# The product of two weight matrices of a one-head attention layer, as seven products of half-size blocks

## The chip, the cores and the metric

The kernel runs on one core of a Trainium2 chip. The metric is device microseconds of one execution. A core has a matrix engine (TensorE, PE in the profile; its weight loads are listed as PEld), VectorE (DVE), ScalarE (ACT), GpSimd (POOL), and SyncE (SP), which here only issues transfers (DMA). Each engine takes its own instructions in order and waits on semaphores for the others. Before the change the kernel took 2408.46 us, the median of 3 runs (2408.44 to 2410.81).

## The reference

Four layers act on x (4 images, 512 channels, 32 x 32 positions, so 1024 tokens each), all in float32:

- layer 0: attention with 8 heads of 64, an output projection, and x added;
- layer 1: linear attention (softplus of queries and keys), a gate from the maximum and the mean of x, and x added;
- layer 2: layer norm over channels, attention with one head of 512, an output projection, and x added;
- layer 3: group norm, attention with 4 heads of 128, an output projection, and x added.

The change is in layer 2, whose core is

```
xn = (xf - mu) * rsqrt(var + EPS) * norm_w
q, k, v = split(xn @ w_qkv.T + b_qkv)
out = softmax(q @ k.T * scale) @ v
out = out @ w_proj.T + b_proj
return x + out
```

With one head, the value and the output weights can be multiplied once, ahead of all tokens: out = softmax(..) @ (xn @ W) with the 512 x 512 matrix W = (w_proj @ w_v).T. Query and key weights can be put together in the same way. Both are done in the kernel.

## The kernel before, in words

plain_path computes everything for one image after another, layer by layer; 512 x 512 matrices are kept as 4 chunks of 128 partitions. PE's order of work is written out by hand (manual_schedule, line 1754): the order of the program text is PE's order. The other engines' order comes from a scheduler that places each instruction by priority and by when its inputs are expected, with two means to steer it: soon() (line 679) raises the priority of what it encloses, and issue_after(i) lets instructions follow instruction i.

**Seven products.** Large matrix products are made from seven half-size block products instead of eight, with sums before and after. seven_products (line 728) holds the scheme. The sums of one operand, the "weights", are made by block_sums or sum_weights (lines 718 and 708), four tensor operations on POOL (lines 711, 712, 714, 715). The sums of the other operand, the "inputs", are made by sum_inputs (line 698), four operations on DVE: L701 the first sum, L702 the second, which needs the first, L703 the third, and L704 the fourth. sum_inputs also records its last instruction in summed[0]. The products are p1 to p7. p1 and p2 need no sums; ACT copies their results out (L763, L768, or L770 with a bias). p6 needs the second sum of both operands, p7 the third, p5 the first, p4 the fourth; the results of p3 to p7 are joined on DVE: L791 (p6), L797 (p7) and L754 or L756 (p5, p4 and p3). The order is p1 and p2 of the output blocks, then for each pair of blocks p6, p7, p6, p5, p4, p7, p3, p5, p4, p3. A matmul with float32 operands shows as two PE instructions in the trace.

**Slots.** Other work is threaded between products: pieces is a list of small functions, and each call of slot() runs the next one; idle is a function that does nothing and takes a slot. later is a list of work with a countdown in ticks; tick() counts it down. layer_norm (line 1578) and linear_attention (line 1389) return such lists of pieces.

**Around the change** (lines 1804 to 1858). Layer 0 of the last image has just ended; the last image's layer 1 and the first image's layer norm are still to be done, and they are interleaved with two products of weights:

1. gq, the product of the query and key weights: four times fold (line 1804: four matmuls 128 x 128 x 512 that add up in one PSUM bank; PE line L654), then a copy by ACT (L1846). Three of the folds come early, the fourth here. After the third and the fourth copy there is a slot.
2. hv, the product of the value weights (the last third of w2) and the output weights wo2: four folds (L654, "acc<-wo,w" in the trace), each with a copy by ACT (L1853) and a slot.
3. two weighted biases, uq and bo2 (weighted_bias, line 550; DVE line L559), which issue_after(summed[0]) puts after the last instruction of the sums made last.
4. the first image's layer 2: the query product with gq (seven_products with two slots, "acc<-ln,gq" and "acc<-w,ws" on PE line L724), then the product of the tokens with hv (project_v), then the attention (one_head).

The pieces in the slots are: the rest of the layer norm of the first image (the reciprocal L1614 and the scaling L1619 of its first half; centering L1597, squares on ACT L1602, their sum L1606, and the matmul that adds over channels L1611 of its second half), the gate of the last image (gates: on DVE a maximum over all tokens, L1418, on ACT four sums, L1421), its features (two matmul groups, L654 "feat<-x,block" and L1404), the transposes of its tokens (L1437 on DVE, then transfers to squares and from there to l, L1445 and L1451 on SP), and so on. L1103 is the end of layer 0 of the last image on DVE. Line 1830 loads a copy of half an image for the second image's layer norm.

Buffers: PSUM has four one-bank tiles (acc) and two two-bank tiles (sc). The POOL sums of seven_products lie in the two buffers of tag "sum". The tag "os" has one buffer; it holds sums of layer 0's output weights until layer 0 is over, and later sums of layer 2's queries.

Of the kernel before, what the change touches and what calls it, by code (L numbers as in the profile page):

```python
# [13 lines left out]
F32 = mybir.dt.float32  # L14
# [4 lines left out]
P = 128  # L19
B = 4  # L20
C = 512
S = 1024
NC = C // P
# [452 lines left out]
def plain_path(ctx: ExitStack, tc: tile.TileContext, d: dict, out: bass.AP, count):  # L476
# [11 lines left out]
    nc = tc.nc  # L488
# [4 lines left out]
    work = ctx.enter_context(tc.tile_pool(name="work", bufs=1))  # L493
# [6 lines left out]
    def acc_tile():  # L500
        return ps_acc.tile([P, TB], F32, tag="acc", name="acc")
# [24 lines left out]
    def chunks_tile(tag, name, bufs=1):  # L526
        return work.tile([P, NC, TB], F32, tag=tag, bufs=bufs, name=name)
# [7 lines left out]
    def load_wo(src):  # L535
        t = wpool.tile([P, NC, C], F32, tag="wo", name="wo")
        nc.sync.dma_start(t, src.rearrange("(c p) o -> p c o", p=P))
        return t
# [112 lines left out]
    def product(ps, lhs, rhs):  # L651

        for c in range(NC):
            nc.tensor.matmul(ps, lhsT=lhs(c), rhs=rhs(c), start=(c == 0), stop=(c == NC - 1))  # L654
# [3 lines left out]
    later, pieces = [], []  # L658
# [7 lines left out]
    def tick():  # L666
        for item in later:
            item[0] -= 1
        while later and later[0][0] <= 0:
            later.pop(0)[1]()  # L670

    def slot():
        tick()
        if pieces:
            pieces.pop(0)()

    idle = lambda: None
# [20 lines left out]
    def sum_inputs(tiles, inputs):  # L698

        t = tiles  # L700
        nc.vector.tensor_tensor(t[0], inputs(0, 1), inputs(0, 0), ALU.subtract)  # L701
        nc.vector.tensor_tensor(t[1], inputs(1, 1), t[0], ALU.subtract)  # L702
        nc.vector.tensor_tensor(t[2], inputs(1, 1), inputs(0, 1), ALU.subtract)  # L703
        last = nc.vector.tensor_tensor(t[3], inputs(1, 0), t[1], ALU.subtract)  # L704
        summed[:] = [last.ins]
        return t
# [16 lines left out]
    def tokens_moving(ps, w, x, m, o, start, stop):  # L723
        nc.tensor.matmul(  # L724
            ps, lhsT=w[:, m, :], rhs=x[:, m, :], start=start, stop=stop, skip_group_check=True
        )
# [152 lines left out]
    def project_qkv(wqkv, bias, src, vt, room, first=False, between=lambda: None):  # L879

        q = q_tiles()
        k = work.tile([P, NC, S], F32, tag="k", name="k")
        inputs = lambda j, tb: src(tb)[:, 2 * j : 2 * j + 2, :]
        made = []

        def sums():
            with tc.issue_after(closing.pop()) if closing else nullcontext():
                made.extend(sum_inputs([pt_tile("t") for _ in range(4)], inputs))
            return made


        seven_products(
            NC,
            lambda i, j, o: wqkv[:, 2 * j : 2 * j + 2, i * C + o * P : i * C + (o + 1) * P],
            inputs,
            lambda i, o: col(bias, i * NC + o),
            lambda i, tb, o: k[:, o, bass.ts(tb, TB)] if i else q[tb][:, o, :],
            sums,
            slots=1,
            first=first,  # L900
        )

        assert len(pieces) <= 7
        wv = wqkv[:, :, 2 * C :]
        between()
        project_v(vt, wv, inputs, made, room())
        return q, k

    def output_sums(wo):

        t = work.tile([P, 4, NC // 2, C // 2], F32, tag="os", bufs=1, name="os")
        return sum_weights(
            [t[:, i] for i in range(4)],
            lambda i, j: wo[:, 2 * j : 2 * j + 2, i * C // 2 : (i + 1) * C // 2],
        )
# [838 lines left out]
    with tc.manual_schedule(engines={mybir.EngineType.PE}):  # L1754


        ps = acc_tile()
# [11 lines left out]
        for b in range(B):  # L1769
            vt = v_tiles()  # L1770
            if b > 0:
                pieces.extend(linear_attention(b - 1, lambda i: vt[i]))
            q, k = project_qkv(
                wqkv0, "bqkv0", lambda tb: xs[b][:, :, bass.ts(tb, TB)], vt,
                lambda: chunks_tile("ot", "ws"), first=(b == 0),
                between=outputs_bias,
            )
# [7 lines left out]
            if b == 0:  # L1785
                os = output_sums(wo0)
            if b == B - 1:
                w2 = wpool.tile([P, 3 * NC, C], F32, tag="wqkv", name="w2")
# [15 lines left out]
        def fold(ps, left, right, o):  # L1804
            product(ps, lambda c: w2[:, left + c, bass.ts(o, P)], lambda c: right[:, c, :])
# [19 lines left out]
        wo2 = load_wo(d["wo2"])  # L1825
# [15 lines left out]
        for o in range(NC):  # L1841
            ps = gps.get(o)
            if ps is None:
                ps = acc_tile()
# [2 lines left out]
            if o >= NC // 2:  # L1847
                slot()
        hv = w2[:, :NC, :]
        for o in range(NC):  # L1850
            ps = acc_tile()
            fold(ps, 2 * NC, wo2, o)
            nc.scalar.copy(hv[:, o, :], ps)  # L1853
            slot()

        with tc.issue_after(summed[0]):
            uq = weighted_bias("uq", loadedq)
# [5 lines left out]
        for b in range(B):  # L1863
# [18 lines left out]
            def sums():  # L1882
# [12 lines left out]
                slots=2,  # L1895
            )

            pair = lambda t, i: t[:, 2 * i : 2 * i + 2, :]
# [42 lines left out]
        for b in range(B):  # L1941
            vt = v_tiles()

            q, k = project_qkv(
                wqkv3, "bqkv3", lambda tb: ready[tb], vt,
                lambda: wpool.tile([P, NC, C], F32, tag="wo", name="ws") if b == 0
                else chunks_tile("ot", "ws"),
            )
            if b == 0:
                wo3 = load_wo(d["wo3"])  # L1950
                os = output_sums(wo3)
# [17 lines left out]
@with_exitstack  # L1969
def conv_seq(ctx: ExitStack, tc: tile.TileContext, d: dict, out: bass.AP):  # L1970
    nc = tc.nc
    flag = ctx.enter_context(tc.tile_pool(name="flag", bufs=1))
    count = flag.tile([1, 1], mybir.dt.int32, name="count")
    plain_path(tc, d, out, count)
    good = nc.values_load(count, min_val=0, max_val=P)  # L1975
    with tc.If(good < P):
        general_path(tc, d, out)
# [56 lines left out]
```

## Time and profile before

| | us |
|---|---|
| median of 3 runs | 2408.46 (2408.44 to 2410.81) |
| the profiled execution, time | 2407.96 |
| its span in the profile | 2406.2 |
| PE busy | 2396.1 |
| DVE busy | 1505.6 |
| ACT busy | 702.1 |
| POOL busy | 245.9 |
| first instruction of hv's product (L654, acc<-wo,w) | 935.02 |
| first instruction of the query's product after it (L724) | 953.42 |

Times are microseconds from the start of the span unless marked ns. A row of the timeline gives start, length, engine, source line, operation, what is written and read, the shape, the number of instructions merged, and in square brackets idle time before it with what ended it. A row of the waits gives who waited for whom, the total, the number of times and the longest. A window's row gives its length, then for each engine the busy time and the number of instructions, then the granted PE clock (1.00 is full), the share of DMA time and GB/s. Matmul ends are modelled: rows of matmuls that follow each other overlap by about 0.17 us in this list, so the pace is read from start to start. Each fence in the text is one view of the profile.

### The profile page before, as it was taken

To read this page: it belongs to the slowest core of one execution; us is meant where nothing else is said; L and a number is where in the kernel's file an instruction comes from. 1 tells how busy PE (TensorE), PEld (TensorE's weight loads), DVE (VectorE), ACT (ScalarE), POOL (GpSimd) and SP (SyncE) were. 2 spreads that over 40 slices of the span, in tenths; PEclk is the share of its full clock that TensorE was granted. 3 is DMA by queue.
4 is the path that set the end of the run, shared out by engine and by line. 5 is a ranking of instruction groups with operands and counts; after the bars stand their busy time and mean duration, and the time that the engine had idled before them with its cause. 6 is when DMAs were issued, how large, how long until landed. Compare 5 with 4: busy or idle time off the path is not lost. (4 is left out here: it accounts for less than half of the span.)

```text
span 2406.2 us, 24706 instructions
## 1 busy us (share of the span) xinstructions
PE 2396.1 (100%) x10014; PEld 1197.0 (50%) x10014; DVE 1505.6 (63%) x1834; ACT 702.1 (29%) x866; POOL 245.9 (10%) x240
## 2 busy tenths in 40 slices
PE   9999999999999999999999999999999999999999
PEld 5444544453445344544646445455556446455653
DVE  3678577757875789685585865654563554445344
ACT  1454154315531653230302202013321330331132
POOL 4001100110020001102102021011020001002000
PEclk9999999999999999999999999999999999999999
DMA  6001220212021213111002020110010001000001
GB/s 188 10 10 36 57 80 10 62 31 80 19 62 63 100 37 95 64 66 79 18 9 79 22 87 0 62 70 18 36 70 1 22 31 53 0 35 36 0 25 43
DMA packets 45895, 112.28 MB, mean 47 GB/s; under 512 B 3807, under 2 KB 21215, under 8 KB 42830
## 3 DMA queue, kind: packets, MB, share of 16 engines
q1 hardware_dynamic: 45774, 110.64, 13.7%
q8 instruction: 80, 1.31, 0.2%
q14 instruction: 41, 0.34, 0.0%
HBM read 75.79 MB, written 33.78 MB: 46 GB/s over the span
## 5 line engine op out<-in xcount | busy, mean ns | idle before, releaser
L958 ACT ACTIVATE pt<-sc 128x1024 f32<-128x1024 f32 x384 | 379.6, 1022 | 531.4 <-PE sc L953 303.9
L967 DVE TENSOR_TENSOR sum<-sum,pt 128x1024 f32<-128x1024 f32 x256 | 314.5, 1229 | 160.8 <-ACT pt L958 147.5
L984 PE MATMUL acc<-pt,v 64*64 64x512 f32 x2048 | 245.7, 591 | 0.0
L948 PE MATMUL sc<-q,k 64*64 64x512 f32 x2048 | 243.8, 591 | 1.1 <-ACT pt L958 1.1
L999 PE MATMUL acc<-pt,v 128*128 128x512 f32 x512 | 240.8, 594 | 0.0
L953 PE MATMUL sc<-q,k 128*128 128x512 f32 x512 | 239.8, 593 | 0.0
L724 PE MATMUL acc<-t,ws 128*128 128x512 f32 x384 | 173.9, 593 | 0.0
L711 POOL TENSOR_TENSOR ws<-wqkv 128x256 f32<-128x256 f32 (+1 forms) x40 | 39.2, 981 | 1289.9 <-PE acc L1035 513.3
L964 DVE TENSOR_TENSOR sum<-pt 128x1024 f32<-128x1024 f32 x64 | 78.0, 1219 | 137.0 <-ACT pt L958 137.0
L999 PEld LDWEIGHTS acc<-pt,v 128*128 128x128 f32 x512 | 96.6, 190 | 125.3 <-issue 121.6
L953 PEld LDWEIGHTS sc<-q,k 128*128 128x128 f32 x512 | 96.8, 190 | 116.2 <-issue 92.9
L984 PEld LDWEIGHTS acc<-pt,v 64*64 64x64 f32 x2048 | 76.8, 133 | 143.9 <-issue 141.5
L948 PEld LDWEIGHTS sc<-q,k 64*64 64x64 f32 x2048 | 76.4, 133 | 141.8 <-issue 132.9
L724 PEld LDWEIGHTS acc<-t,ws 128*128 128x128 f32 x384 | 72.7, 190 | 88.1 <-issue 86.3
L763 ACT COPY v<-acc 128x512 f32<-128x512 f32 x24 | 14.1, 586 | 305.1 <-PE acc L849 305.1
L693 DVE RECIPROCAL rd<-acc 128x512 f32<-128x512 f32 (+1 forms) x25 | 83.8, 3353 | 29.1 <-PE acc L1035 29.1
L763 ACT COPY q<-acc 128x512 f32<-128x512 f32 x40 | 23.4, 586 | 221.1 <-PE acc L724 221.1
L849 PE MATMUL acc<-ws,t 128*128 128x256 f32 x384 | 87.1, 380 | 0.0
L1095 PE MATMUL acc<-ot,wo 128*128 128x256 f32 x360 | 85.4, 382 | 1.7 <-DVE ot L1068 1.7
L856 PE MATMUL acc<-q,ln 128*128 128x512 f32 x192 | 86.6, 594 | 0.0
L856 PE MATMUL acc<-qs,w 128*128 128x512 f32 x192 | 86.5, 592 | 0.0
L754 DVE TENSOR_TENSOR v<-acc,v 128x512 f32<-128x512 f32 x72 | 49.7, 690 | 53.1 <-PE acc L849 53.0
(321 smaller groups left out, 3392.6 us busy)
## 6 DMA issues: line engine op xcount, KB each, us to landing
home<-x SPq DMA_DIRECT2D x8, 2048.0 KB
x<-home SPq DMA_DIRECT2D x8, 2048.0 KB
rds<-quotients SPq DMA_DIRECT2D x32, 256.0 KB
squares<-squares SPq DMA_DIRECT2D x32, 256.0 KB
out<-x SPq DMA_DIRECT2D x31, 256.0 KB
rds<-quotients SPq DMA_DIRECT2D x7, 1024.0 KB
x<-in_x SPq DMA_DIRECT2D x3, 2048.0 KB
v<-squares SPq DMA_DIRECT2D x12, 512.0 KB
```

Of the source, the lines that this page charges most:

```text
L693: nc.vector.reciprocal(rd, ps)
L724: nc.tensor.matmul(ps, lhsT=w[:, m, :], rhs=x[:, m, :], start=start, stop=stop, skip_group_check=True)
L849: nc.tensor.matmul(ps[:, bass.ts(r, C // 2)], lhsT=x[:, m, bass.ts(2 * o + r, P)], rhs=w[:, m, :], start=(start and r == 0), stop=stop, sk ...
L856: nc.tensor.matmul(ps, lhsT=x[:, m, bass.ts(o, P)], rhs=w[:, m, :], start=start, stop=stop, skip_group_check=True,)
L948: nc.tensor.matmul(ps[half(h), s, :], lhsT=key(g, i)[half(s), half(h)], rhs=q[qb][half(s), g, :], start=True, stop=True,)
L953: nc.tensor.matmul(ps[:, s, :], lhsT=key(g, 2 * i + s), rhs=q[qb][:, g, :], start=True, stop=True)
L958: exps.append(nc.scalar.activation(pt, ps, AF.Exp, scale=scale).ins)
L964: adds.append(nc.vector.tensor_tensor(acc, pts[n - 1], pt, ALU.add).ins)
L967: adds.append(nc.vector.tensor_tensor(acc, acc, pt, ALU.add).ins)
L984: nc.tensor.matmul(outs[qb, g][r][half(s), :], lhsT=v[i // 2][half(r), i % 2, g * P + s * hd : g * P + (s + 1) * hd], rhs=pt[half(r), s, : ...
L999: nc.tensor.matmul(outs[qb, g][0], lhsT=v[j // 2][:, j % 2, bass.ts(g, P)], rhs=pt[:, s, :], start=(j == 0), stop=(j == NT - 1),)
L1095: nc.tensor.matmul(ps[i][:, bass.ts(o, n)], lhsT=w[:, m, bass.ts(o, P)], rhs=t[:, m, :], start=(start and m + o == 0), stop=(stop and m == ...
```

## The change

The four folds of hv are replaced by a call of seven_products. The weights operand is the value part of w2, in 128 x 128 blocks (sums on POOL, 128 x 256 elements for each of two output blocks); the inputs operand is wo2, split in halves by rows and by columns, so that the moving side of a matmul has 256 columns. The four sums of wo2 go to a new tile fsums in the buffer of tag "os" (L701 to L704 on DVE, 128 x 512 elements each). There is no bias, so p1 and p2 are copied by ACT (L763, L768) and the rest are joined by DVE with 128 x 256 elements each (two L791, two L797, six L754). PE does 28 matmuls of 256 columns instead of 16 of 512.

The slots are one in the first part and five in the second, six where there were four; two idle pieces are put into the list, so the other pieces up to there are the same. Since sum_inputs sets summed[0], the weighted biases uq and bo2 now follow the sums of wo2; before, summed[0] was an instruction of layer 0.

In the order of instructions the first transpose (L1437) of the second pair now stands on DVE ahead of the maximum L1418, the sums of wo2 stand between the additions of the squares (L1606), and the bias rows L559 stand after the sums. On PE the feature matmuls (L654, "feat<-x,block") stand after p1, p2 and the first p6, p7, p6, p5; before, they stood after the second fold. On SP the load of line 1830 stands ahead of the four loads L1451; before, it stood after them. On POOL the eight sums of the value weights stand ahead of the sums of gq.

```diff
         hv = w2[:, :NC, :]
-        for o in range(NC):
-            ps = acc_tile()
-            fold(ps, 2 * NC, wo2, o)
-            nc.scalar.copy(hv[:, o, :], ps)
-            slot()
+
+        pieces[1:1] = [idle]
+        pieces[3:3] = [idle]
+        n, pair = C // 2, NC // 2
+        fsums = work.tile([P, 4, pair, n], F32, tag="os", bufs=1, name="fs")
+        columns = lambda tb: slice(tb * n, (tb + 1) * n)
+        inputs = lambda j, tb: wo2[:, pair * j : pair * (j + 1), columns(tb)]
+        seven_products(
+            pair,
+            lambda i, j, o: w2[
+                :, 2 * NC + pair * j : 2 * NC + pair * (j + 1), bass.ts(i * pair + o, P)
+            ],
+            inputs,
+            None,
+            lambda i, tb, o: hv[:, i * pair + o, columns(tb)],
+            lambda: sum_inputs([fsums[:, k] for k in range(4)], inputs),
+            None,
+            lambda ps, *args: tokens_moving(ps[:, :n], *args),
+            lambda ps: ps[:, :n],
+            slots=1,
+        )
 
         with tc.issue_after(summed[0]):
             uq = weighted_bias("uq", loadedq)
             bo2 = weighted_bias("bo2", loadedv)
```

## The prediction

> **What bounds the kernel now.** I read the engine totals first, then the waits of the matrix engine (PE), then the busy time of each engine stage by stage around the edited lines, then the timelines of PE and of VectorE (DVE) there. The totals, and the only row of PE's waits between 926 and 1000 us:
>
> ```profile
> PE 2396.1 (100%) x10014; PEld 1197.0 (50%) x10014; DVE 1505.6 (63%) x1834; ACT 702.1 (29%) x866; POOL 245.9 (10%) x240
> ```
> ```profile
> PE acc L724 <- DVE w L702: 0.4, 1, 0.4
> ```
>
> PE is busy for the whole span, and its waits in the whole program are five rows that add up to 4.5 us. So a delay of PE anywhere is handed on to the end: hardly any idle time later can take it up. DVE's average of 63% hides the stage that is edited. Two windows (length, then busy time of PE, weight load, DVE, ACT, POOL, then clock, DMA share, GB/s):
>
> ```profile
> 934.00:954.00 20.00, 19.89 (x47) 8.61 (x46) 20.00 (x25) 9.46 (x18) 5.13 (x8) 1.00 0.00 0
> 954.00:965.00 11.00, 10.57 (x33) 3.79 (x32) 11.00 (x11) 4.62 (x7) 5.09 (x4) 1.00 0.57 142
> ```
>
> From 934 to 965 us DVE is busy for 31.0 of 31 us, and PE too, but for the 0.4 us that it waits for DVE at the end. The timelines there (start, length, engine, line), first PE's, then DVE's:
>
> ```profile
> 935.02 7.03 PE L654 MATMUL acc<-wo,w 128*128 128x512 f32 x16
> 941.89 3.60 PE L654 MATMUL feat<-x,block 128*128 128x512 f32 x8
> 945.32 3.60 PE L654 MATMUL acc<-wo,w 128*128 128x512 f32 x8
> 949.03 1.12 PE L1611 MATMUL lnsums<-sq,ones 128*128 128x512 f32 x2
> 949.99 3.60 PE L654 MATMUL acc<-wo,w 128*128 128x512 f32 x8
> 953.42 3.60 PE L724 MATMUL acc<-ln,gq 128*128 128x512 f32 x8
> 956.95 3.65 PE L1404 MATMUL feat<-x,block 128*64 128x512 f32 x16
> 960.53 3.70 PE L724 MATMUL acc<-ln,gq 128*128 128x512 f32 x8
> 964.67 1.53 PE L724 MATMUL acc<-w,ws 128*128 128x512 f32 x3 [0.43 <-DVE w L702]
> ```
> ```profile
> 933.64 4.41 DVE L1418 TENSOR_REDUCE gate<-x 128x4 f32<-128x4096 f32 x1
> 937.97 3.33 DVE L1614 RECIPROCAL rstd<-rstd 128x512 f32<-128x512 f32 x1
> 941.23 0.62 DVE L1597 SCALAR_TENSOR_TENSOR ln<-lnsums,x 128x512 f32<-128x512 f32 x1
> 941.78 2.72 DVE L1619 SCALAR_TENSOR_TENSOR ln<-ln,cols,rstd 128x512 f32<-128x512 f32 x4
> 944.42 1.87 DVE L1597 SCALAR_TENSOR_TENSOR ln<-lnsums,x 128x512 f32<-128x512 f32 x3
> 946.22 0.68 DVE L1606 TENSOR_TENSOR sq<-sq 128x512 f32<-128x512 f32 x1
> ```
>
> The reader is to see that the product of the value and output weights (32 instructions acc<-wo,w; each matmul in the source is two) needs nothing that DVE makes here, so PE works through it while DVE does its reduction, reciprocal and layer norm. It is what PE does while DVE is behind.
>
> **The change part by part.** The sum is made against the profiled execution: 2407.96 us, of it 2406.2 us span; it stands 0.5 us under the median of the runs, 2408.46.
>
> *PE's own work.* Removed: 32 instructions of 512 columns; 16 run from 935.02 to 941.89, 0.43 us each: 13.7 us. Added: 7 products x 2 output blocks x 2 matmuls x 2 = 56 instructions of 256 columns. Rows of that form (L849) give 0.226 us each (16 from 984.57 to 988.22, 16 from 994.97 to 998.53): 12.7 us. Gain: 1.1 us.
>
> *DVE's added work.* Four sums of wo2 (L701 to L704, 128x512) at a pitch of 0.60 us, as rows of that shape start at 928.87, 929.47, 930.08: 2.4 us. Ten joins of 128x256 from PSUM, which the trace does not have: 128x256 rows in SBUF last 0.42 us (L1308), 0.34 of pitch if they overlap as the others do; 128x512 joins last 0.69 at 0.60 of pitch. Between 3.4 and 6.0 us for ten; I take 3.5, as the work goes by elements. Together 5.9 us, on an engine without a free microsecond. At most 1.6 comes back: L563 (four numbers) lasts 1.11 us and one L559 row 1.21 instead of 0.68, both beside POOL's work, which moves.
>
> *What is queued ahead of the sums.* This decides. In the changed kernel's instruction order the first sum (L701) stands on DVE behind the last L1103, one stream transpose (moved up), the reduction, the reciprocal, one L1597, four L1619, three L1597 and one L1606; the third product, p6, needs the second sum (L702). The four L559 that ran between 928.26 and 933.64 now stand behind the sums, because issue_after(summed[0]) now names the last sum of wo2. So the last two L1103 follow the PE product that ends at 930.03, and are through at 931.3 rather than 933.03. Then the transpose, 1.16 (950.73 to 951.89 before): 932.45. Reduction 4.33: 936.8. Reciprocal 3.26: 940.05. L1597, L1619, L1597 as in the rows above, 0.55 + 2.64 + 1.80: 945.05. L1606, L701, L1606, L702 at 0.60: 947.45. p6 can start at about 947.55.
>
> *When PE gets there.* p1 and p2 begin at 935.02, as the old product did: 16 instructions, 3.6 us. p2 waits for ACT's copy of p1, which stands behind two L1421 rows that end at 937.1: 0.8 us. PE is through at 939.4 and stands still until 947.55: **8.15 us**. The feat product (3.4 us) can't fill this, since PE takes its products in order and feat comes after four of the DVE-fed ones.
>
> *From there on.* p6 0.9; p7 waits 0.25 for the third sum, 948.7; p7, p6, p5 2.7: 951.4. feat 3.44: 954.9. Four products 3.6: 958.5. L1611 0.9 and two products 1.8: 961.15. There the query's product starts, 953.42 before. It takes 10.8 us to its own p6: 971.95. DVE's second reciprocal waits for L1611 and runs from 960.3 to 963.55; two joins 0.7, four L1619 2.6 to 3.8 (the latter beside POOL's work), L701, L703, L702 3.4: 970.3 to 971.5. DVE is just in time, so the 0.43 us go: 971.95 against 964.67, **+7.3 us**.
>
> *The clock.* PE's last work ends at 2400.8. What the granted clock (last column but two) does then, and the kernel's first matmul, in the form of grouped instructions (busy, mean ns):
>
> ```profile
> 2403.00:2404.00 1.00, 0.00 (x0) 0.00 (x0) 0.00 (x0) 0.00 (x0) 0.00 (x0) 1.00 0.12 35
> 2404.00:2405.00 1.00, 0.00 (x0) 0.00 (x0) 0.00 (x0) 0.00 (x0) 0.00 (x0) 0.84 0.00 0
> 2405.00:2406.00 1.00, 0.00 (x0) 0.00 (x0) 0.00 (x0) 0.00 (x0) 0.00 (x0) 0.50 0.05 16
> ```
> ```profile
> L724 PE MATMUL acc<-x,wqkv 128*128 128x512 f32 x1 | 1.2, 1191 | 0.0
> ```
>
> After 3.9 us without work the clock is half. The first matmul lasts 1191 ns, later ones 592, and they do so from about 5 us, 3.9 us after PE's first work at 1.12. So the wait should halve the clock, and 3.9 us of work at half speed lose 1.95 us, less 0.25 for p7's wait, which they cover: **+1.7 us**. Bounds: nothing if the clock stays, 3.4 if the slow stretch is twice as long.
>
> [...]
>
> *What costs nothing.* POOL's eight added sums (128x256, 0.72 us each, 5.8 in all) need only w2 and buffers that L1035 has left by 904; POOL has been idle for 206 us there; without that cover they would follow gq's first copy at 931 and end at 937, still before 947. gq's own sums move behind the last products (961) and are through by about 965, needed from 971.95; without that slack they would cost their 2.9 us. SP: L1830 (1 MB of x) moves ahead of the four L1451 loads; all wait for the squares after the second transpose, which ends at 957.05 (957.39 before), while PE is 7 us later; uncovered, the 1 MB would take some 4 us. ACT has four 128x256 copies for four 128x512.
>
> Sum: waits 8.15 + 0.8 + 0.25, less 1.1 of work, less the 0.43 and 0.36 that PE waits in this stretch now: 7.3. With the clock **+9.0 us**: 2417.0 for a profiled execution, 2417.4 against the median.
>
> **The rivals.**
> 1. *The clock stays, or its loss is hidden*: the waits alone, +7.3, 2415.8. For it: the clock falls only 3.9 us into the gap. Against: it would be half when work comes back.
> 2. *DVE is late a second time.* With the slow clock, L1611 and with it the second reciprocal come 1.7 us later, and DVE has the query's sum at 972.0 to 973.2, PE wants it at 973.65. Joins at 0.60 (+2.5) put DVE last, and more where POOL's sums run beside it: 2 to 3.5 us more, about 2420.
> 3. *Not slower.* DVE gets to the sums early. wo2 has landed by 934; if L701 and L702 ran ahead of the reduction, p6 would not wait, PE would keep 1.1 - 0.8 us, and what is left is DVE's 5.9 - 1.6 = 4.3 us ahead of the query's sum, or nothing if the bias rows go behind it: 2408.2 to 2412.7. It decides from an L702 that ends by 943.3, a gap too short for the clock and +3.0 in all. Against it: the order puts L701 behind the reduction and the reciprocal, 7.6 us, and the rows above show DVE taking them without a gap.
>
> **How the numbers follow.** Forecast 0.55, rival 1 0.20, rival 2 0.17, rival 3 0.08. A measurement can't tell less than 0.2% (4.8 us, up to 2413.3) from no change. Rival 3 gives 0.06 of same and 0.02 of faster; all else is slower, 0.92. The range reaches from 2414.2 (+5.7: rival 1, if DVE also gets its 1.6 us back ahead of the sums) to 2420.8 (rival 2, and the clock's upper bound, +12.4): it leaves out rival 3 and the tail of rival 2.
>
> **What the changed profile would show.** A wait of about 8 us of PE L724 for DVE fs L702 near 947; DVE's L701 on fs at about 945.6, behind the reduction; a granted clock under 1 around 944 to 951 and the first 256-column instructions near 0.43 us apart; the query's product at about 963; all later stages as long as before. I would be wrong with no such wait (rival 3), with a wait at a clock of 1.00 (rival 1), or with a second wait of L724 for w (rival 2).

## The result, and the profile after

The changed kernel takes 2422.73 us, the median of 6 runs (2420.23 to 2423.25), against 2408.53 us for the kernel before (6 runs, 2408.28 to 2410.81): a ratio of 1.0056, 95% interval 1.0046 to 1.0067. That is 14.2 us slower. The forecast was 9.0 us slower, 2417.4, with a range of 2414.2 to 2420.8: the direction was right, the size outside the range. The profiled execution took 2422.85 us, its span 2420.7 us.

The rows of PE's waits for the edited stretch. There was one of 0.4 before; now there are three.

```profile
PE acc L724 <- DVE fs L702: 8.2, 1, 8.2
PE acc L724 <- DVE w L702: 2.9, 1, 2.9
PE acc L724 <- ACT w L763: 0.6, 1, 0.6
```

The timeline of PE after the change, p6 to p5 of the new product, the query's first products, and the query's p6 to p5:

```profile
948.17 6.35 PE L724 MATMUL acc<-fs,ws 128*128 128x256 f32 x16 [8.20 <-DVE fs L702]
954.36 3.60 PE L654 MATMUL feat<-x,block 128*128 128x512 f32 x8
...
963.84 3.60 PE L724 MATMUL acc<-ln,gq 128*128 128x512 f32 x8
...
977.57 8.74 PE L724 MATMUL acc<-w,ws 128*128 128x512 f32 x16 [2.92 <-DVE w L702]
```

This execution is 0.44 us later than the one before when the stretch begins (first L1595 at 934.60 against 934.16). The query's product then starts at 963.84, where it started at 953.42: 10.0 us later, net of the 0.44. Its own p6 waits once more, for 2.92 us, and its 16 instructions take 8.58 us to the next row (986.15) instead of 6.94. Windows of 1 us show why both groups of 16 are long (clock in the last column but two):

```profile
943.00:944.00 1.00, 0.00 (x0) 0.00 (x0) 1.00 (x3) 0.00 (x0) 0.00 (x0) 0.66 0.00 0
...
953.00:954.00 1.00, 1.00 (x5) 0.86 (x4) 0.48 (x3) 0.00 (x0) 0.00 (x0) 0.72 0.00 0
...
977.00:978.00 1.00, 0.43 (x1) 0.46 (x2) 1.00 (x2) 0.00 (x0) 0.00 (x0) 0.73 0.00 0
...
980.00:981.00 1.00, 1.00 (x3) 0.34 (x1) 0.00 (x0) 0.98 (x2) 0.00 (x0) 0.56 0.00 0
```

All windows between the first and the second, and between the third and the fourth, have 0.50. A window of mean 0.66 at levels of 1 and 0.5 means that the clock fell 0.32 us into it. So it fell at 943.32, 3.35 us after PE's last work (939.97), and came back at 953.56, 5.4 us after work resumed. It fell a second time at 977.46, after 2.8 us without work, and came back at 980.88, 3.3 us after work resumed. The last section shows what these moments have in common.

The timeline of DVE after the change, at its two late arrivals:

```profile
946.13 0.69 DVE L701 TENSOR_TENSOR fs<-wo 128x512 f32<-128x512 f32 x1
...
947.34 0.69 DVE L702 TENSOR_TENSOR fs<-wo,fs 128x512 f32<-128x512 f32 x1
...
963.03 3.35 DVE L1614 RECIPROCAL rstd<-rstd 128x512 f32<-128x512 f32 x1 [1.15 <-ACT rstd L1613]
...
967.78 4.09 DVE L1619 SCALAR_TENSOR_TENSOR ln<-ln,cols,rstd 128x512 f32<-128x512 f32 x3
971.79 2.29 DVE L701 TENSOR_TENSOR w<-ln 128x1024 f32<-128x1024 f32 x1
974.01 2.28 DVE L703 TENSOR_TENSOR w<-ln 128x1024 f32<-128x1024 f32 x1
976.21 1.21 DVE L702 TENSOR_TENSOR w<-ln,w 128x1024 f32<-128x1024 f32 x1
```

The first arrival is as worked out: net of the 0.44, L701 starts at 945.69 and L702 at 946.90, for 945.65 and 946.85 in the forecast. At the second, the four L1619 take 4.9 us from start to start, and L701 and L703 2.2 each. In the kernel before the same rows were

```profile
957.32 3.80 DVE L1619 SCALAR_TENSOR_TENSOR ln<-ln,cols,rstd 128x512 f32<-128x512 f32 x4
961.04 1.21 DVE L701 TENSOR_TENSOR w<-ln 128x1024 f32<-128x1024 f32 x1
962.18 1.21 DVE L703 TENSOR_TENSOR w<-ln 128x1024 f32<-128x1024 f32 x1
```

POOL's timeline beside them after the change, the first and the third of four sums of the tokens' product (project_v), and then the first and the last of the same four before it:

```profile
967.94 1.71 POOL L711 TENSOR_TENSOR ws<-w 128x512 f32<-128x512 f32 x1 [0.96 <-DVE w L754]
...
971.28 1.72 POOL L712 TENSOR_TENSOR ws<-ws,w 128x512 f32<-128x512 f32 x1
```
```profile
953.73 1.27 POOL L714 TENSOR_TENSOR ws<-w 128x512 f32<-128x512 f32 x1 [13.64 <-issue]
...
957.65 1.60 POOL L715 TENSOR_TENSOR ws<-w,ws 128x512 f32<-128x512 f32 x1
```

These sums read hv, and the code puts them into the buffer of wo2. Before, they began when PE had read wo2 for the last time (its last fold ends at 953.6), ACT's last copy of hv was done by 954.21, and they ran from 953.73 to 959.25: beside the end of the reciprocal, L563, a transpose and the first of the four L1619, at 1.26 to 1.28 us each for the first three. Now hv is whole only with the last join L754 (967.45 to 967.86), and that join stands on DVE behind the second reciprocal. So they begin 14 us later, beside the rows that the query waits for.

The account up to the first matmul of L1314, in the attention that follows, at 1085.02 after and 1070.58 before: 14.4, less the 0.44, is 14.0. Waits 8.20 + 0.64 + (2.92 - 0.43); the first group of 16 took 6.19 to the next row for 3.62 at the forecast's pace, 2.57 (the slow clock and p7's wait); the second 8.58 instead of 6.94, 1.64; less 1.08 of work at the same pace, and less the 0.36 by which PE's rows from 935.02 to 953.42 before stand further apart than their work (18.40 for 18.04). Sum: 14.1.

### The profile page after: what moved, and what is told of

The parts are those of the page before. It is cut to its first block, busy times and chain, and to the rows that moved or that the text cites. A ratio compares the mean times of both kernels' runs of the same rounds, so it can differ in the third digit from the quotient of the medians.

```text
span 2420.7 us, 24782 instructions
## 1 busy us (share of the span) xinstructions
PE 2399.1 (99%) x10038; PEld 1203.8 (50%) x10038; DVE 1513.5 (63%) x1848; ACT 701.1 (29%) x866; POOL 253.9 (10%) x248
## 3 DMA queue, kind: packets, MB, share of 16 engines
q8 instruction: 81, 1.33, 0.2%
## 5 line engine op out<-in xcount | busy, mean ns | idle before, releaser
L763 ACT COPY v<-acc 128x512 f32<-128x512 f32 x24 | 14.1, 586 | 305.6 <-PE acc L849 305.6
L763 ACT COPY q<-acc 128x512 f32<-128x512 f32 x40 | 23.4, 586 | 222.7 <-PE acc L724 222.7
L849 PE MATMUL acc<-ws,t 128*128 128x256 f32 x384 | 87.1, 380 | 0.0
L754 DVE TENSOR_TENSOR v<-acc,v 128x512 f32<-128x512 f32 x72 | 49.8, 691 | 53.1 <-PE acc L849 53.0
```

The lines of the kernel that those rows point to most:

```text
L849: nc.tensor.matmul(ps[:, bass.ts(r, C // 2)], lhsT=x[:, m, bass.ts(2 * o + r, P)], rhs=w[:, m, :], start=(start and r == 0), stop=stop, sk ...
```

## The experiments

Each run is compared with runs of the kernel before on the same chip. Medians of before: 2408.79 us for the first four experiments, 2408.40 for the next four, 2408.24 for the last two. Single runs of one kernel spread by up to 3.3 us (experiment 1), so differences of a microsecond or two between medians are read together with the traces.

**1. The clock kept up.** Between p2 and p6, PE does nine products of 512 columns whose result nobody reads.

```diff
+        def busy():
+            ps = two_tile("busy")[:, 0, :]
+            for _ in range(9):
+                nc.tensor.matmul(ps, lhsT=ones, rhs=wo2[:, 0, :], start=True, stop=True)
+        pieces[0:1] = [both(pieces[0], busy)]
```

> The changed kernel with nine matmuls of 512 columns more (18 PE instructions, 7.7 us at full clock) between p2 and p6 of the weight product. They read wo2 and a matrix of ones, write a PSUM tile that nobody reads, and so fill the 8.2 us in which PE waits for the sums of wo2 without making anything later. Theory (the idle halves PE's clock, and the slow stretch after it costs 2.6 us of its own): the granted clock stays 1.00 from 940 to 956, the first sixteen 256-column instructions after the wait take 3.6 us instead of 6.2, L1611 comes 2.6 us earlier, and DVE's and POOL's chains behind it with it, so the second wait stays near 2.9 us: 2420.1 us. Rival (DVE alone sets the time through this stretch, the slow clock lies beside its bias rows and joins): what PE gains is added to the second wait, which grows to about 5.5 us, and the time stays at 2422.7 us.

Measured: 2420.24 us (2418.51 to 2421.76), ratio 1.0046 (1.0029 to 1.0063). PE's timeline in this run:

```profile
948.15 3.97 PE L724 MATMUL acc<-fs,ws 128*128 128x256 f32 x16 [0.47 <-DVE fs L702]
951.95 3.60 PE L654 MATMUL feat<-x,block 128*128 128x512 f32 x8
...
975.16 10.11 PE L724 MATMUL acc<-w,ws 128*128 128x512 f32 x16 [2.92 <-DVE w L702]
```

p6 starts at 948.15 as in the changed kernel, and feat follows 3.80 us later instead of 6.19: the slow clock of the first gap costs 2.4 us there, and 2.5 by the medians. The wait for the query's sum stays at 2.92: that wait does not come from the slow clock of the first gap, as PE and DVE move together. The slow clock behind the second gap cost this execution 3.1 us (10.11 against 7.03 at full clock), more than the 1.6 of the changed kernel, so its own time, 2421.76, is the highest of the four.

**2. POOL held back.** A one-column POOL operation reads the query's fourth sum (L704), and the four sums for project_v follow it.

```diff
...
+            if b == 0:
+                probe = small.tile([P, 1], F32, tag="probe", bufs=1, name="probe")
+                last = made[3][:, 0, :1]
+                held = tc.issue_after(nc.gpsimd.tensor_tensor(probe, last, last, ALU.add).ins)
+            with held:
+                project_v(
...
```

> The changed kernel with POOL's four sums of hv for the first image's value product (128x512, L711 to L715) held back until DVE has made the fourth sum of the query's inputs (L704): a one-column POOL operation reads that sum, and the four are queued behind it. Theory (the second wait comes from POOL and DVE working side by side: L1619, L701 and L703 take about twice their usual time there): L1619 at 0.66 to 0.7 us each, L701 and L703 at 1.2 us instead of 2.3, the sum L702 about 4 us earlier, before PE wants it, so the second wait (2.9 us) and the slow clock after it (1.6 us) both go: 2418.2 us. Rival (those DVE rows are slow for another reason, or DVE is late by its order alone): the rows keep their lengths, a second wait of 2 to 3 us stays, 2422.7 us, or more by what the later POOL sums cost the value product.

Measured: 2418.31 us (2417.86 to 2418.46), ratio 1.0040 (1.0026 to 1.0054). DVE's timeline in this run, the rows that answer to those at 967.78 and 971.79:

```profile
967.38 2.06 DVE L1619 SCALAR_TENSOR_TENSOR ln<-ln,cols,rstd 128x512 f32<-128x512 f32 x3
969.37 1.21 DVE L701 TENSOR_TENSOR w<-ln 128x1024 f32<-128x1024 f32 x1
```

The rows are half as long, the query's p6 starts at 974.09 without a wait and at full clock, and 4.4 us are gone. So the second wait, and the second fall of the clock with it, come from POOL's sums beside DVE. (A wait of 0.24 for the keys is new; experiment 7 says where it comes from.)

**3. The features' product between p2 and p6**, so that PE has work in the first gap.

```diff
-        pieces[1:1] = [idle]
-        pieces[3:3] = [idle]
+        pieces[0:2] = [both(*pieces[0:2]), idle, idle, idle]
```

> The changed kernel with the first feature matmuls (8 instructions, 3.4 us) put into the slot after p2, ahead of p6, so that real work fills part of the first wait. Theory: the first wait shrinks from 8.2 to 4.8 us; the clock still falls, 3.8 us after the last feature instruction, so the slow stretch stays; L1611 comes 3.4 us earlier, but DVE then still has its bias rows and joins to do and gains only some 2 us, and the second wait grows to between 3 and 4.5 us: 2419.3 to 2421 us. Rival (the first wait alone is the loss): all 3.4 us come back, 2419.3 us, and with a clock that stays up 2416.7 us.

Measured: 2419.14 us (2418.88 to 2419.40), ratio 1.0043 (1.0027 to 1.0060). The first wait is 4.77 instead of 8.20, as feat's 3.4 us now lie in it; the group of 16 takes 5.21 to the next row, 1.4 more than the 3.80 of experiment 1. The query's p6 starts at 973.10, 4.5 us earlier than in the changed kernel, but there the wait is 3.25, and its group takes 9.91 instead of 8.74. So 3.6 us are gone, and the loss at the query's sums is not among them. The time is the rival's, 2419.3, and just under the range of the theory; the second wait grew as the theory had it, but only by 0.33, and the first group lost 1.0 less than in the changed kernel (5.21 to the next row instead of 6.19).

**4. The sums of wo2 ahead of the reciprocal.** This is what rival 3 rests on.

```diff
+        def sums_early():
+            with tc.high_priority(offset=2000):
+                t = sum_inputs([fsums[:, k] for k in range(4)], inputs)
+            return t
...
-            lambda: sum_inputs([fsums[:, k] for k in range(4)], inputs),
+            sums_early,
```

> The changed kernel with the four sums of wo2 given a high priority, so that DVE has L701, L703 and L702 ahead of the reciprocal, directly behind the maximum L1418, and the joins come earlier too. Theory (the place of the sums in DVE's queue makes the first wait): L702 ends at about 939.5, p6 starts with a wait under 1 us, no slow clock; then the squares' sum L1606 and with it L1611 is late on DVE instead, a wait of about 2 us, and the second reciprocal follows the bias rows, so that the query's product waits 1 to 4 us for L702 beside POOL: 2411 to 2416 us. Rival (DVE's 5.9 us of added work is the loss, wherever it stands): the first wait moves whole into later waits, 2420 us or more.

Measured: 2420.26 us (2419.35 to 2421.52), ratio 1.0049 (1.0033 to 1.0066). p6 no longer waits. PE's waits in this run:

```profile
PE acc L724 <- DVE w L702: 4.7, 1, 4.7
PE lnsums L1611 <- DVE sq L1606: 4.6, 1, 4.6
```

What DVE does early, it does not do for the squares and for the query: two other waits of PE take the place of the first, and the time is less by only 2.5 us. The theory had 2411 to 2416; the rival, 2420 or more, is what came.

**5. Both: sums early, POOL held back** (the diffs of 4 and 2 together).

> The changed kernel with both moves at once: the four sums of wo2 ahead of the reciprocal on DVE, and POOL's four 128x512 sums held until DVE is through with the query's fourth sum (L704). Theory (what is lost is DVE's added work, and POOL running beside DVE lengthens it): no wait of L724 for fs; the wait of L1611 for sq stays at about 4.6 us, as it is DVE's own work ahead of it; L1619 and L701 go back to about 0.66 and 1.2 us each, so the wait of 4.7 for w falls under 1.5 us and its slow clock stretch goes: 2414 to 2416.5. Rival (POOL is incidental, the query's sums are late because DVE has had more to do): the wait for w keeps 3 us or more, 2418.5 to 2420.3.

Measured: 2415.14 us (2414.34 to 2417.47), ratio 1.0029 (1.0018 to 1.0041). The wait of L1611 is 4.59 still, and its two instructions take 2.08 instead of 1.02, so PE is slow after it; the wait for the query's sum is 0.61. So even with the order of rival 3 and without POOL beside the query's sums the kernel stays 6.7 us slower. Not all of that is DVE's added work: PE also waits 1.12 us for the keys (L1462), which comes from holding POOL back (experiments 7 and 10), and 1.5 us are slow clock behind the 4.59.

**6. The kernel before with DVE's added work alone.** PE's product stays the old one; on DVE the four sums of wo2 and ten additions of 128x256 are done, and nobody reads them.

```diff
...
             nc.scalar.copy(hv[:, o, :], ps)
+            if o == 0:
+                keep = summed[0]
+                sum_inputs([fsums[:, k] for k in range(4)], inputs)
+                summed[0] = keep
+            for k in range((2, 2, 3, 3)[o]):
+                half = hv[:, o, (k % 2) * n : (k % 2 + 1) * n]
+                nc.vector.tensor_tensor(junk, half, half, ALU.add)
             slot()
```

> The kernel before with DVE's added work alone: the four sums of wo2 are made and ten additions of 128x256 on hv that nobody reads are done on DVE between the folds; PE's instructions are those of before, and nothing waits for the added work. Theory (5.9 us on a DVE that had no free microsecond, with a rise beside POOL): L1611 late by 1 to 2.4 us and the query's second sum late by 3 to 6 us in all: 2412 to 2416. Rival (the loss is made by the product's dependence on the sums and by its form on PE, while DVE can take the work in the time that the bias rows and small rows give back): 2408 to 2410.

Measured: 2415.49 us (2414.94 to 2417.30), ratio 1.0028 (1.0017 to 1.0039), 7.1 us slower than before. PE's timeline and then DVE's, in this run:

```profile
972.71 9.20 PE L724 MATMUL acc<-w,ws 128*128 128x512 f32 x16 [5.62 <-DVE w L702]
```
```profile
958.04 1.31 DVE L1865 TENSOR_TENSOR junk<-w 128x256 f32<-128x256 f32 x1
959.28 1.75 DVE L1619 SCALAR_TENSOR_TENSOR ln<-ln,cols,rstd 128x512 f32<-128x512 f32 x1
960.96 1.49 DVE L1865 TENSOR_TENSOR junk<-w 128x256 f32<-128x256 f32 x1
```

This execution reaches the stretch 2.5 us late (first L1595 at 936.69), so its starts can't be set directly against those of before. 5.9 us of work on the full DVE come back as 5.2 us more of wait for the query's sum and 0.4 at L1611; the gap then costs 2.2 us of slow clock (9.20 against 7.03). Two of the additions, 0.41 each elsewhere, take 1.31 and 1.49 beside POOL's sums (956.58 to 962.2), so about 2 us of this belong to POOL. These additions read SBUF alone, while the joins have one input in PSUM. The scheduler's order changed too: L1381 and three of the bias rows now stand ahead of the query's L702, both transposes L1437 behind it. No product in seven blocks is needed for a loss of this size: the load on DVE, in the order that the scheduler gives it, is enough.

**7. The sums of wo2 on POOL, and POOL's later sums held back.** POOL has nothing to do from 907.6 on; its first sum of wo2 starts at 934.45, when wo2 has arrived. The diff of 2 is in this kernel too.

```diff
-            lambda: sum_inputs([fsums[:, k] for k in range(4)], inputs),
+            fsums_on_pool,
...
+        def fsums_on_pool():
+            t = [fsums[:, k] for k in range(4)]
+            tt = nc.gpsimd.tensor_tensor
+            tt(t[0], inputs(0, 1), inputs(0, 0), ALU.subtract)
...
+            return t
```

> The changed kernel with the four sums of wo2 on POOL, which is idle there, in place of DVE, and POOL's sums for the tokens' product held until L704. DVE then has only ten joins more than before, 3.5 us. Theory: p6 does not wait (POOL has the second sum by about 939), the clock stays, DVE's joins show as a wait of 1 to 2 us at L1611 or of 1 to 2 us for w, against 1.1 us less work on PE: 2407.5 to 2411. Rival (even ten joins on the full DVE cost more than they take, or POOL's sums slow DVE's maximum and reciprocal): 2413 or more.

Measured: 2411.14 us (2410.46 to 2412.89), ratio 1.0011 (1.0002 to 1.0021). PE's waits:

```profile
PE keys L1462 <- DVE block L1387: 1.8, 1, 1.8
...
PE acc L724 <- DVE w L702: 1.4, 1, 1.4
PE lnsums L1611 <- DVE sq L1606: 1.3, 1, 1.3
```

p6 doesn't wait, its group takes 3.45 to the next row (939.93 to 943.38), and 11.5 of the 14.2 us are gone. Ten joins still cost two waits of 1.3 and 1.4. The 1.8 for the keys is new, since POOL's sums now stand beside L1383 to L1386 (1.51, 1.80 and 1.69 us, and 0.67, 1.20 and 1.21 in experiment 10), steps of the softplus on DVE that the keys' transpose (L1462) waits for; with it the time lies just above the 2407.5 to 2411 of the theory.

**8. The kernel before with POOL's sums held back** (the diff of 2 alone).

> The kernel before with POOL's four 128x512 sums held until DVE is through with L704. Theory: the four L1619 take 2.7 us instead of 3.8 and the four-number L563 about 0.1 instead of 1.11, DVE is 2 us earlier at the query's second sum, and the only wait there, 0.43 us, goes: 2407.9 to 2408.6. Rival: POOL's later sums delay the tokens' product or slow the joins of the query: 2409.5 or more.

Measured: 2407.76 us (2407.33 to 2408.43), ratio 0.9997 (0.9987 to 1.0006): no difference that can be told. The rows of L1619 are shorter there too (2.70 instead of 3.80 for four) and the 0.43 us wait is gone, with 0.28 at the keys in its place. Before the change the neighbourhood of POOL and DVE cost next to nothing.

**9. Clock kept up and POOL held back** (1 and 2 together): what is left should be the forecast's sum without its clock term.

> The changed kernel with both things that the forecast missed or mis-sized taken out together: nine dummy products of 512 columns between p2 and p6 that keep the clock up, and POOL's four 128x512 sums held until L704. The dummy products lie in the wait for the sums, so the output is the same. Theory (what is left is the forecast's sum without its clock term, +7.3 us, and the two loss terms add): no slow clock in 934 to 980, no wait for w, 2415.0 to 2416.5. Rival (the two terms overlap, or a third loss lies under them): 2417.3 or more, with another wait of PE in the stretch.

Measured: 2415.82 us (2415.24 to 2417.51), ratio 1.0032 (1.0020 to 1.0044). PE's timeline:

```profile
961.13 3.60 PE L724 MATMUL acc<-ln,gq 128*128 128x512 f32 x8
...
971.78 7.03 PE L724 MATMUL acc<-w,ws 128*128 128x512 f32 x16
```

The forecast had 961.15 and 971.95 for these two rows, and DVE's L702 at 970.3 to 971.5; it ends at 970.54. The two losses add: 2.5 and 4.4 apart, 6.9 together.

**10. As 7, with POOL's sums held until the features are done**: the probe reads what L1387 writes.

```diff
...
-                last = made[3][:, 0, :1]
+                last = soft[0][:, :1]
...
```

> The changed kernel with the sums of wo2 on POOL, and POOL's four 128x512 sums held until the last instruction of the features (L1387) in place of L704. Theory (POOL beside L1383 to L1387 is what makes the keys' wait of 1.8 us in the run that held them to L704): that wait falls under 0.6 us and the time by 1.2 to 1.8 us, to 2409.3 to 2410. Against the kernel before it is then 0.9 to 1.6 us slower: the waits for L1611 and w, 1.3 and 1.4, outweigh the 1.1 us of work saved. Rival: POOL's sums now come late for the tokens' product, or slow the joins after L1387 instead: 2411 or more.

Measured: 2410.09 us (2409.42 to 2412.16), ratio 1.0008 (0.9999 to 1.0017). The keys' wait is 0.26; 1.30 at L1611, 1.36 for the query's sum and 0.64 for ACT's copy remain, against 1.08 of saved work. This is the best form of the change that was run, and it isn't faster than the kernel before.

## Why the prediction was right in direction and wrong in size

- *PE's own work, 1.1 less.* Close. The pace of 0.226 was that of L849 in the kernel before; the new rows stand 0.216 apart at a clock of 1.00 (four from 957.80 to 958.66), and a group of 16 takes 3.46 in experiment 4. So 56 rows take 12.1 and not 12.7, 1.6 less than the old product. But at the two pauses the starts lie 0.4 further apart than rows and waits (10.19 from p2 to p6, for 1.73 of rows and 8.20 of wait, and 2.53 from p1 to p2, for 1.73 and 0.64), which leaves 1.2.
- *DVE's added work, 5.9 us.* Right: the joins last 0.42 at a pitch of 0.33 to 0.34, the sums 0.60. Put alone into the kernel before (experiment 6), a load of this size costs 7.1 us, of which some 2 belong to POOL beside the additions and 2.2 to the slow clock.
- *What is queued ahead of the sums, and when PE gets there.* Right within 0.2 us: L702 on fs at 946.90 net of the 0.44, for 946.85, the wait 8.20 for a forecast of 8.15, ACT's 0.64 for 0.8. Experiment 9 brings out the whole chain to the query's p6, 971.78 against 971.95, and the sum of 7.3 as 7.6.
- *The clock, +1.7.* The clock fell to 0.50 in the gap, as forecast, but the term was mis-sized: it came back 5.4 us after work resumed and not 3.9, so the first stretch cost 2.4 (2.5 by experiment 1). Both times differ from gap to gap. The falls came 3.9 us after PE's last work at the end of the kernel before, 3.35, 2.8 and, at its end, 2.65 us in the changed one (2415.23 to 2417.88), and 3.0 in experiment 6 (967.1 to 970.1); the returns came 5.4 and 3.3 us after work resumed in the changed kernel, 4.2 in experiment 6 (972.71 to 976.94) and, as an estimate from the 3.1 us that it lost at half speed, some 6 in experiment 1. So one gap, read once at the end of the kernel, could not give this term.
- *"DVE is just in time, so the 0.43 us go."* This step failed, and with it the cover under *What costs nothing*, where POOL's sums for project_v weren't followed. The step priced the four L1619 up to 3.8 beside POOL; they took 4.9, and L701 and L703, priced with L702 at 3.4 together, took 1.1 more each. The changed kernel's last writer of hv is a DVE join behind the reciprocal, and that puts POOL's 7 us of sums on these rows. DVE arrived at 977.4 (977.0 net of the 0.44), not at 972.0 to 973.2 (with the slow clock). The wait of 2.92 was long enough for a second fall of the clock: 2.92 + 1.64 in place of nothing. Experiment 2 shows the cause by taking it away. L1619, L701 and L703 take about twice what they take without POOL there (4.09 for three L1619 against 2.06, 2.29 against 1.21), while a join, with one input in PSUM, keeps its length beside POOL (L797 at 978.31 in experiment 2, 0.68).
- *The rivals.* Rival 2, at 0.17, is what happened. Of its two reasons POOL's sums were the one, and not slow joins, which kept the pitch of 0.33; its price of 2 to 3.5 holds the wait (2.92) and leaves out the second fall of the clock (1.64). Rival 1 is ruled out by the windows. Rival 3 named the wrong price: with the sums early and POOL out of the way the kernel is at 2415.14, not at 2408.2 to 2412.7, because the squares for L1611 are then late by 4.6 us, a wait that it left out, as it did the slow clock behind it.
- *Sums that don't come out.* Rival 2 and the clock's upper bound together are 7.3 + 3.4 and 2 to 3.5 more, so 12.7 to 14.2 and not the 12.4 that ends the range: added up, these two would have reached the 14.2 that was measured. Rival 3 ends at 2412.5 by its own terms (0.3 less, 4.3 more), not at 2412.7. The sums of gq are eight and not four: they ended at 966.98, not at about 965, and no wait of PE comes from them.
- *What it adds up to.* 2417.4 plus 2.9 for the second wait, 1.6 for the second slow stretch and 0.7 for the first is 2422.6; measured 2422.73.

## What to carry to other kernels

A product split to save 8% of its matmul time gives the work to the engine that makes its sums and joins. Where that engine has no free microsecond, as DVE here, most of the added work comes back as waits of PE (5.6 us for 5.9 in experiment 6, 2.2 for the 3.5 of the joins in experiment 10), and reordering mostly chooses which instruction waits. When the writer of a result changes from one engine to another, follow every reader of that result: the time at which the readers start changes too, and what then runs beside them. A gap of about 3 us on PE should be priced with its slow clock, as a range for each gap: the waits of 2.9 to 3.3 us for the query's sum cost 1.6 to 3.1 us more here (the changed kernel and experiments 1 and 3). Behind the waits of 1.3 to 1.8 us in experiment 7 the rows kept their pace (6.94 us for the query's p6 to the next row, as in the kernel before).

## What the runs showed of the hardware that was not expected

- Some rows of POOL and DVE were longer side by side than alone. POOL's 128x512 sum takes 1.27 to 1.29 us in experiment 10 (all four) and 1.71 in the stretch above; DVE's 128x1024 sum 1.21 alone and 2.29 beside POOL, its 128x512 L1619 has a pitch of 0.66 alone and 1.33 beside POOL, and L563, on four numbers, takes 0.12 alone and 1.11. These rows have two inputs in SBUF. L1383, one input and a constant, was slowed too: 0.69 alone, 1.78 in experiment 2. L1385, two inputs in SBUF, took 1.80 in experiment 7, but 1.23 in experiment 2, where POOL's sum beside it took 2.25. The reciprocal kept its length (3.31 beside POOL's sums in the kernel before, 3.34 without POOL in the changed one), and so did joins, with one input in PSUM (L797 0.68 beside POOL in experiment 2, 0.69 without at 982.92 in the changed kernel).
- In the changed kernel and in experiment 6 the moments at which PE's clock changed lie whole numbers of 3.41 us apart. The four of the changed kernel (943.32, 953.56, 977.46, 980.88) are 10.24, 23.90 and 3.42 apart: 3, 7 and 1 steps; the two of experiment 6 (970.10, 976.94, read in the same way) 6.84: 2 steps. If the time is cut into such steps ahead of and behind each moment, the clock fell after steps with little work of PE in them: 0.06 and 0.60 us in the changed kernel, 0.40 in experiment 6, 1.27 in experiment 1 (970.97 to 974.38). It stayed low after steps with 1.98 (changed kernel, 946.73 to 950.14), 0.81 (experiment 6, 970.10 to 973.52) and 2.63 (experiment 1, 974.38 to 977.79), and came back after 3.31 (changed kernel, 977.46 to 980.88) and after two steps full of work (to 953.56, and to 976.94 in experiment 6). Two waits of the same 2.92 us so cost 1.6 and 3.1 us: in the changed kernel the clock fell 0.11 us before work resumed and was back after one step, in experiment 1 it fell 0.78 us before and is still 0.50 in the window from 978 to 979.
